# Layer 0's first expert block moved into the plan of the first stage (two-layer adaLN kernel with routed experts, one core)

## The chip, the cores and the metric

The kernel runs on one core of one Trainium2 chip. The metric is the device time of one execution in microseconds; the time given for a kernel is the median of several runs.

## The reference, cut to what matters

Two layers, each with a modulated layer norm, a mixing step, a second modulated layer norm and a feed-forward step that sends each token to two of eight experts. The change concerns the feed-forward step of layer 0:

```python
h = _layernorm(x, axis=-1) * (1 + cb) + sb          # x is (4, 1024, 256)
logits = jnp.einsum('bsd,de->bse', input_emb, Wr) + br
route_w = jax.nn.softmax(logits, axis=-1)
_, topk_idx = jax.lax.top_k(route_w, TOP_K)          # TOP_K = 2 of E = 8
...
h = jax.nn.relu(jnp.einsum('bsd,edh->ebsh', input_emb, W1) + b1[:, None, None, :])
expert_out = jnp.einsum('ebsh,ehd->ebsd', h, W2) + b2[:, None, None, :]
return jnp.einsum('bse,ebsd->bsd', routed, expert_out)
```

All is float32; D is 256, the hidden width H is 1024.

## The kernel before, in words

**First stage.** Tokens lie in tiles of 128 rows. For four batches the kernel does layer 0's norms and mixing and the routing; normed rows are stored to a table in device memory, `h_rows`, with two more columns for where a row's result goes (`store` and `mark` in `second_half`, plan pieces of SyncE, L1310 and L1323, with planned costs of 4.0 and 1.0).

**Sorting the pairs.** A token and one of its experts is a pair. Pairs of an expert fill blocks of 128 rows; there are at most 71 blocks. At the end of the first stage `total_staged` (L558) sums pairs by expert on TensorE; `close_staged` (L585) turns these totals on VectorE into numbers of blocks and the expert of each block; `across` (L685) spreads them over partitions with one product on TensorE; `limits` (L690) and `list_weights` (L716) make from that the bounds of every block and the list of weight rows. Which 128 rows are a block's is found by `reach` (L746, VectorE), `look` (L761, TensorE) and `find` (L774, VectorE); `fetch` (L791) then gathers those rows from `h_rows` with an indirect DMA that GpSimd issues. Block 0 needs no closing: `begin` (L577) gives its bound from the bases alone. Its expert is always the last one, whose weights lie in the buffers from early on.

**A block** is: gather the rows, two transposes on TensorE (`turn_rows`, L1675), a copy of the result from PSUM (`rows_turned`, L1681, VectorE), eight tiles of 128 hidden features in two groups of four (`hidden`, L1692, TensorE), each group followed by four relu with bias on ScalarE (`rectified`, L1707), eight products that sum into one PSUM tile (`values`, L1717), the bias (`biased`, L1730, VectorE) and a scatter of the rows (`kept`). Weights come in by indirect gathers (`weights_in`, `weights_out`), two buffers each, one block ahead; they are skipped when the buffer has the expert already.

**What sets the order.** Each engine runs its instructions in the order in which the program gives them. In the first stage that order is a planner's (class `Plan`, L41): each piece has an engine, a planned cost in microseconds, pieces that it comes after, slots that it holds (PSUM and SBUF buffers) and a rank. The planner steps through planned time and gives each free engine the ready piece of lowest rank; a piece from another engine counts 0.12 later; `lag` is added to a piece's end for those that wait on it. It may hold a piece back for one of a much lower rank that is ready soon. Pieces are then emitted in the order of their planned starts. `kept_busy` (L919) adds filler products on TensorE whose result nobody reads, of the highest ranks: three after look(0), five after across, three after look(1).

**The loop.** After the plan, blocks run in a loop written out by hand (L1781): in pass j the weights of block j+1, the scatter of block j-2, the gather of block j+2, `reach` for j+3, `hidden` and `rectified` for block j, transposes and copy for block j+1, `look` and `find` for j+3, then `values` and `biased` of block j-1. Ahead of it stand the gathers of blocks 0 and 1 and the transposes and copy of block 0.

In the first stage's tail the pieces are, in the code's order (L1398 to L1437):

```python
d = plan(DVE, 3.9, lambda: g0.close_staged(pa), after=[m], holds=[ps], rank=-1.0)
...
begun = plan(DVE, 0.3, g0.begin, after=[bs], rank=-1.6)
...
r = plan(DVE, 0.5, reach, after=[d] if j else [begun], rank=first)
m = plan(PE, 0.25, look, after=[r], holds=[ps], rank=first)
plan(DVE, 0.6, find, after=[m], holds=[ps], rank=first if j else -0.95)
```

Of the kernel before, what the change touches and what calls it, by code (L numbers as in the profile page):

```python
# [8 lines left out]
F32 = mybir.dt.float32  # L9
F16 = mybir.dt.float16  # L10
I32 = mybir.dt.int32
AF = mybir.ActivationFunctionType
ALU = mybir.AluOpType
# [6 lines left out]
P = 128  # L20
B, S, D = 4, 1024, 256
NC = S // P
KD = D // P
E = 8
# [115 lines left out]
def adaln_d2_kernel(  # L140
# [218 lines left out]
    class Pairs:  # L359
# [222 lines left out]
            )  # L582
            nc.vector.tensor_copy(self.nth[:, 0:1], lane)

        def close_staged(self, scratch):  # L585


            J, blocks, runs, origin, up1 = self.J, self.blocks, self.runs, self.origin, self.up1
            begin2 = float(J - LATE)

            def t(shape, what, dt=F32):
                return scratch.tile(shape, dt, tag=f"g_{what}", name=f"g_{what}", bufs=1)

# [4 lines left out]
            )  # L598
            blocks_i = t([P, 2, E], "blocks_i", I32)
            nc.vector.tensor_scalar(blocks_i, whole, 7, None, ALU.logical_shift_right)  # L600
            nc.vector.tensor_copy(blocks[:, :, 1:], blocks_i)

            up = t([P, 2, E + 1], "up")
            nc.vector.tensor_tensor_scan(
# [299 lines left out]
    sT1 = silu_of(1, c1)  # L904
    gate_rows = pa.tile([B, 2, D], F32, name="gate_rows", bufs=1)

    plan = Plan(p1=3, p2=2, pm=3, xn1=5, h1T=2, xn2=6, h2T=2, t1=1, le=2)
    PE, ACT, DVE, POOL = "PE", "ACT", "DVE", "POOL"
    tiles = {}
# [299 lines left out]
    def second_half(b):  # L1209
# [73 lines left out]
        for gs in routed:  # L1283
            k, at = 4 * len(gs), 4 * gs[0] * B + b
            tag = (b, gs[0])

            def route(k=k, at=at, tag=tag):
                g0.route(pa, tiles["pl", tag[0], tag[1]][:, :, :E], br_sb, at, k, B)

            d = plan(  # L1290
                DVE,
                0.24 * 14 + 0.16 * 4 if k == NC else 0.22 * 14,
                route,
                after=[ready[g][0] for g in gs],
                holds=[ready[gs[-1]][1]],
                rank=rank - 0.2,
            )
            for g in gs:
                of_batch["route", b, g] = d

            def mark(k=k, at=at):
                first = at - at % B
                nc.sync.dma_start(
                    h_rows[first * P : (first + k * B) * P, D:].rearrange(
                        "(c b p) d -> b p c d", b=B, p=P
                    )[at % B],
                    g0.meta[:, at : at + (k - 1) * B + 1 : B, :],
                )

            plan("SP", 1.0, mark, after=[d], rank=rank)  # L1310
            for g in gs:
                back, slot, key = backs[g]

                def store(g=g, key=key):
                    at = 4 * g * B * P
                    nc.sync.dma_start(
                        h_rows[at : at + 4 * B * P, :D].rearrange(
                            "(c b p) d -> b p c d", b=B, p=P
                        )[b],
                        tiles["xn", key],  # L1320
                    )

                plan("SP", 4.0, store, after=back, holds=[slot], rank=rank)  # L1323


    ps = plan.slot("p1")
# [75 lines left out]
        tiles["bases"] = g0.bases(ps_1)  # L1402

    m2 = plan(PE, 0.2, bases, after=[d], holds=[ps2], rank=-1.6)
    d = plan(DVE, 3.9, lambda: g0.close_staged(pa), after=[m], holds=[ps], rank=-1.0)
    bs = plan(
        ACT,
        0.25,
# [3 lines left out]
        rank=-1.6,  # L1412
    )
    begun = plan(DVE, 0.3, g0.begin, after=[bs], rank=-1.6)
    ps = plan.slot("p1")
    m = plan(PE, 0.4, lambda: g0.across(ps_1), after=[d], holds=[ps], rank=-1.0)
    kept_busy(1.1, [m], 30.0)
    d = plan(DVE, 1.4, lambda: g0.limits(pa), after=[m, bs], holds=[ps], rank=-1.0)
    plan(DVE, 1.2, lambda: g0.list_weights(pa), after=[d], holds=[ps], rank=-0.75)
    for j in range(AHEAD):  # L1420
        ps = plan.slot("p1")

        def reach(j=j):
# [8 lines left out]
        first = -1.0 + 0.1 * j if j else -1.6  # L1432
        r = plan(DVE, 0.5, reach, after=[d] if j else [begun], rank=first)
        m = plan(PE, 0.25, look, after=[r], holds=[ps], rank=first)
        plan(DVE, 0.6, find, after=[m], holds=[ps], rank=first if j else -0.95)
        if j < AHEAD - 1:
            kept_busy(0.7, [m], 30.0 + j)  # L1437
    with tc.manual_schedule(engines=ORDERED):
# [233 lines left out]
            ts.append(plan(ACT, 0.67, out_, after=[m], holds=[ps, slotT], rank=rank - 0.03))  # L1672
        return slot, slotT, hs, ts

    def turn_rows(j):  # L1675
        pt = psum(ps_m, [P, KD, P], "pm_x")
        for k in range(KD):
            nc.tensor.transpose(pt[:, k, :], xgbuf[j % 4][:, k * P : (k + 1) * P], ident)  # L1678
        return pt

    def rows_turned(pt):  # L1681
        xT = work.tile([P, KD, P], F32, tag="xT", name="xT", bufs=3)
        nc.vector.tensor_copy(xT, pt)  # L1683
        return xT

    def weights_in(j):
        gather(w1buf[j % 2], W1, g0.wrow[:, j : j + 1], E * P - 1)

    def weights_out(j):
        gather(w2buf[j % 2], W2, g0.wrow[:, j : j + 1], E * P - 1)  # L1690

    def hidden(j, xT, m4):  # L1692
        w1 = w1buf[j % 2]
        p1 = psum(ps_1, [P, 4, P], "p1_h")
        for i in range(4):
            m = 4 * m4 + i
            for k in range(KD):
                nc.tensor.matmul(  # L1698
                    p1[:, i, :],
                    lhsT=w1[:, k * H + m * P : k * H + (m + 1) * P],  # L1700
                    rhs=xT[:, k, :],
                    start=(k == 0),
                    stop=(k == KD - 1),
                )
        return p1

    def rectified(j, hid, p1, m4):  # L1707
        for i in range(4):
            m = 4 * m4 + i
            nc.scalar.activation(  # L1710
                hid[:, m, :],
                p1[:, i, :],
                AF.Relu,
                bias=w1buf[j % 2][:, KD * H + m : KD * H + m + 1],
            )

    def values(j, hid):  # L1717
        w2 = w2buf[j % 2]
        p2 = psum(ps_2, [P, D], "p2_y")
        for m in range(KH):  # L1720
            nc.tensor.matmul(  # L1721
                p2,
                lhsT=hid[:, m, :],
                rhs=w2[:, m * D : (m + 1) * D],
                start=(m == 0),
                stop=(m == KH - 1),
            )
        return p2

    def biased(j, p2):  # L1730
        y = work.tile([P, D], F32, tag="y", name="y", bufs=3)
        nc.vector.tensor_tensor(y, p2, w2buf[j % 2][:, KH * D :], ALU.add)  # L1732
        return y

    dests, ys0 = {}, {}

    def aimed(j):
        dests[j] = g0.aim(work, xgbuf[j % 4], j)

    def kept(j):  # L1740
        put("g0", dests[j], ys0[j])

    def new_hidden():
        return work.tile([P, KH, P], F32, tag="hid", name="hid")


    loads = []
    for k in range(KD):
        loads += [(a[:, k, :], w[k * P : (k + 1) * P, :]) for a, w in ((a0, fw0), (a2, fw2))]
# [24 lines left out]
            nc.sync.dma_start(*loads[j - 8])  # L1774

    with tc.manual_schedule(engines=ORDERED | {EngineType.SP}):
        for j in range(2):
            g0.fetch(xgbuf[j], h_rows, j)
        xT, hid = rows_turned(turn_rows(0)), None
        aimed(0)  # L1780
        for j in range(turning):  # L1781

# [4 lines left out]
                weights_out(j)  # L1787
            g0.fetch(xgbuf[(j + 2) % 4], h_rows, j + 2)
            reached = g0.reach(work, j + AHEAD)
            new = new_hidden()  # L1790
            for m4 in range(2):
                rectified(j, new, hidden(j, xT, m4), m4)

            xT = rows_turned(turn_rows(j + 1))
            aimed(j + 1)
            g0.find(work, g0.look(ps_m, reached), j + AHEAD)
            if j:
                ys0[j - 1] = biased(j - 1, values(j - 1, hid))
            hid = new
            once(j)  # L1800
# [767 lines left out]
```

## Time and profile before

| what | value |
|---|---|
| median of 3 runs | 1121.61 us (1121.43 to 1122.06) |
| the profiled execution: its time | 1141.97 us |
| the profiled execution: its span, first to last instruction | 1140.2 us |
| mean granted TensorE clock | 0.986 |
| TensorE busy | 1086.3 us, 95% of the span |
| VectorE, ScalarE, GpSimd busy | 592.0, 428.6, 422.5 us |
| first stage ends, the loop begins | about 115 us |

All times below are from the profiled execution and count from the start of its span. In the profile PE is TensorE, PEld its weight loads, DVE VectorE, ACT ScalarE, POOL GpSimd, SP SyncE; L12 is line 12 of the kernel. A row of the timeline has start, length, engine, line, operation, what it writes and reads, and in brackets how long the engine had been idle and what ended that. A row of stretches has from and to, its length, then for each engine the busy time and the number of instructions, then the granted clock, the DMA engines' mean busy share and GB/s.

### The profile page before, as it was taken

The numbers are of one execution on the slowest core, as the hardware profiler recorded it, in microseconds if no ns is written. First come the engines' busy times: TensorE is split into PE (matmuls) and PEld (weight loads), VectorE is DVE, ScalarE is ACT, GpSimd is POOL, SyncE is SP. The second block draws the span as 40 slices with busy tenths as digits, with TensorE's granted clock in tenths as the row PEclk, the third lists the DMA queues.
The fourth block names the chain that finished last, engine by engine and source line by source line (L and its number), as shares of the span: only waits on it lengthen the run. The fifth ranks groups of instructions, "written<-read, shape, count | busy, mean of one in ns | idle before, by whom it ended". The sixth has DMA issues, their size and how long they took to land. (4 is left out here: it accounts for less than half of the span.)

```text
span 1140.2 us, 18501 instructions
## 1 busy us (share of the span) xinstructions
PE 1086.3 (95%) x6238; PEld 847.0 (74%) x6238; DVE 592.0 (52%) x2308; ACT 428.6 (38%) x1164; POOL 422.5 (37%) x483
## 2 busy tenths in 40 slices
PE   8998999999999999999999999999999999899883
PEld 5894999999999999999988466566576575547641
DVE  7787232222222222222274788975776445888456
ACT  5976333322333323233343343432434235333421
POOL 1000455555555555555543011010044233616452
PEclk8999999999999999999999999999999999999996
DMA  9414549242422415151260312100024223323532
GB/s 321 174 31 103 191 156 302 100 153 75 154 78 75 150 39 192 33 193 40 70 223 27 96 34 83 39 10 19 19 62 129 75 82 103 102 88 107 155 118 93
DMA packets 77693, 122.38 MB, mean 107 GB/s; under 512 B 27340, under 2 KB 57301, under 8 KB 72990
## 3 DMA queue, kind: packets, MB, share of 16 engines
q0 software_dynamic: 31872, 69.68, 19.5%
q1 hardware_dynamic: 44622, 49.92, 13.3%
q10 hardware_dynamic: 1104, 1.58, 0.4%
q8 instruction: 52, 0.85, 0.3%
q14 instruction: 43, 0.35, 0.1%
HBM read 205.25 MB, written 30.22 MB: 207 GB/s over the span
## 5 line engine op out<-in xcount | busy, mean ns | idle before, releaser
L1710 ACT ACTIVATE hid<-p_h,w 128x128 f32<-128x128 f32 x544 | 154.8, 368 | 323.5 <-issue 251.9
L1698 PEld LDWEIGHTS p_h<-xT,w 128*128 128x128 f32 x2176 | 253.2, 192 | 7.2 <-DVE xT L1683 1.9
L1698 PE MATMUL p_h<-xT,w 128*128 128x128 f32 x2176 | 254.7, 275 | 3.1 <-DVE xT L1683 2.7
L1721 PE MATMUL p_y<-w,hid 128*128 128x256 f32 x1088 | 249.0, 382 | 0.2 <-issue 0.2
L2007 PE MATMUL p_u<-hT,a 128*128 128x512 f32 x512 | 232.0, 596 | 2.9 <-ACT hf L2019 1.4
L1721 PEld LDWEIGHTS p_y<-w,hid 128*128 128x128 f32 x1088 | 201.6, 190 | 25.1 <-DMA w<-in_W,g_wrow 0.4
L2007 PEld LDWEIGHTS p_u<-hT,a 128*128 128x128 f32 x512 | 93.5, 190 | 100.5 <-issue 89.7
L347 POOL DMA_INDIRECT w<-in_W,g_wrow x134 | 135.1, 1008 | 77.4 <-ACT hid L1710 46.7
L1683 DVE COPY xT<-pm_x 128x256 f32<-128x256 f32 x68 | 28.8, 424 | 187.0 <-PE pm_x L1678 134.4
L812 POOL DMA_INDIRECT y<-y,g_dest x68 | 69.5, 1022 | 143.5 <-DVE g_reached L752 108.4
L2055 PE MATMUL p_f<-a,hf 128*128 128x256 f32 x512 | 116.7, 380 | 2.0 <-DVE step L2096 1.0
L1732 DVE TENSOR_TENSOR y<-p_y,w 128x256 f32<-128x256 f32 x68 | 28.9, 425 | 166.9 <-PE p_y L1721 160.7
L2055 PEld LDWEIGHTS p_f<-a,hf 128*128 128x128 f32 x512 | 95.9, 190 | 20.8 <-issue 5.9
L347 POOL DMA_INDIRECT xg<-h_rows,g_row x68 | 66.7, 980 | 120.4 <-DVE g_row L787 98.9
L2103 POOL TENSOR_TENSOR x_sb<-x_sb,step 128x256 f32<-128x256 f32 x32 | 24.9, 778 | 205.8 <-DVE step L2096 153.6
L2315 PE MATMUL p_e<-ew,xT 128*128 x280 | 71.5, 386 | 0.8 <-ACT y L2325 0.8
L2019 ACT ACTIVATE hf<-p_u,decay 128x512 f32<-128x512 f32 x56 | 38.2, 685 | 74.9 <-PE p_u L2007 63.5
L347 POOL DMA_INDIRECT xg<-ga_rows,ga_row x39 | 37.3, 956 | 54.1 <-DVE g_hits L778 19.3
L2315 PEld LDWEIGHTS p_e<-ew,xT 128*128 128x128 f32 x280 | 49.0, 190 | 11.0 <-issue 3.8
L2023 DVE SCALAR_TENSOR_TENSOR hf<-p_u,decay,hf 128x512 f32<-128x512 f32 x56 | 41.9, 748 | 25.7 <-PE p_u L2007 14.3
L1618 DVE TENSOR_TENSOR h<-h,mod 128x256 f32<-128x256 f32 x128 | 51.6, 425 | 6.8 <-ACT h L1608 4.1
L2325 ACT COPY y<-p_e 128x256 f32<-128x256 f32 x70 | 26.1, 373 | 51.4 <-PE p_e L2315 19.2
(371 smaller groups left out, 1259.1 us busy)
## 6 DMA issues: line engine op xcount, KB each, us to landing
yg<-y SPq DMA_DIRECT2D x32, 256.0 KB
ga_y<-y SPq DMA_DIRECT2D x39, 128.0 KB
x_sb<-in_x SPq DMA_DIRECT2D x8, 512.0 KB
h_rows<-xn SPq DMA_DIRECT2D x8, 512.0 KB
gb_y<-y SPq DMA_DIRECT2D x31, 128.0 KB
out_x<-x_sb SPq DMA_DIRECT2D x7, 512.0 KB
a<-in_fw SPq DMA_DIRECT2D x6, 512.0 KB
mod<-mod_rows SPq DMA_DIRECT2D x6, 512.0 KB
```

The source lines that it names most:

```text
L347: return nc.gpsimd.indirect_dma_start(out=dst, out_offset=None, in_=table, in_offset=bass.IndirectOffsetOnAxis(ap=index, axis=0), bounds_c ...
L812: nc.gpsimd.indirect_dma_start(out=table, out_offset=bass.IndirectOffsetOnAxis(ap=dest, axis=0), in_=y, in_offset=None, bounds_check=2 * s ...
L1618: nc.vector.tensor_tensor(h, h, mods1[(sc, sh)[i]][:, b, :], (ALU.mult, ALU.add)[i])
L1698: nc.tensor.matmul(p1[:, i, :], lhsT=w1[:, k * H + m * P : k * H + (m + 1) * P], rhs=xT[:, k, :], start=(k == 0), stop=(k == KD - 1),)
L1710: nc.scalar.activation(hid[:, m, :], p1[:, i, :], AF.Relu, bias=w1buf[j % 2][:, KD * H + m : KD * H + m + 1],)
L1721: nc.tensor.matmul(p2, lhsT=hid[:, m, :], rhs=w2[:, m * D : (m + 1) * D], start=(m == 0), stop=(m == KH - 1),)
L1732: nc.vector.tensor_tensor(y, p2, w2buf[j % 2][:, KH * D :], ALU.add)
L2007: nc.tensor.matmul(pu, lhsT=a[:, k, m * P : (m + 1) * P], rhs=made["n1", c, "hT"][:, k, :, :], start=(k == 0), stop=(k == KD - 1),)
L2019: nc.scalar.activation(made[key, m], made[key, m, 0], AF.Silu, scale=decays[c])
L2023: nc.vector.scalar_tensor_tensor(h, made[key, m, 1], decays[c], h, ALU.mult, ALU.mult)
L2055: nc.tensor.matmul(made[key, "p2", b], lhsT=made[key, m][:, b * P : (b + 1) * P], rhs=a1[:, m, :], start=(m == 0), stop=(m == KH - 1),)
L2315: nc.tensor.matmul(made[key, "p2"], lhsT=made[key, "xT"][:, k, :], rhs=ew_flat[:, bass.ds(made[key, "at"] + k * D, D)], start=(k == 0), st ...
```

## The change

`close_staged` is cut in two: its first three instructions become `whole_blocks`, a piece of its own. `find(0)` gets rank -1.6, and the rest of the closing waits for both. Block 0's gather, transposes, copy (now on ScalarE), hidden products in four pieces, relu in two and values in two become pieces of the first stage's plan (`first_block`); so does block 1's gather. Block 0's gather waits for all stores to `h_rows`. Its hidden tile and transposed rows lie in two buffers of the first stage. The helpers `turn_rows` to `new_hidden` move up in the file; `hidden` and `values` can be given a part. The loop loses what is done already: the two gathers, block 0's transposes, hidden, rectified and values; `biased(0)` stays in pass 1.

```diff
-        def close_staged(self, scratch):
...
+        def whole_blocks(self, scratch):
...
-            nc.vector.tensor_copy(blocks[:, :, 1:], blocks_i)
+            nc.vector.tensor_copy(self.blocks[:, :, 1:], blocks_i)
+
+        def close_staged(self, scratch):
...
-    d = plan(DVE, 3.9, lambda: g0.close_staged(pa), after=[m], holds=[ps], rank=-1.0)
+    whole = plan(DVE, 0.45, lambda: g0.whole_blocks(pa), after=[m], holds=[ps], rank=-1.0)
...
+    def first_block(found):
+
+        slots = [plan.slot("xn1") for _ in range(2)]
+        kept0 = tiles["first"] = {}
+        rows = plan(
+            POOL, 1.0, lambda: g0.fetch(xgbuf[0], h_rows, 0), after=[found, *stores], rank=-1.6, lag=1.9
+        )
+        ps = plan.slot("pm")
+
+        def turn():
+            kept0["pt"] = turn_rows(0)
...
+        m = plan(PE, 0.35, turn, after=[rows], holds=[ps, *slots], rank=-1.5)
+        h = plan(ACT, 0.45, lambda: nc.scalar.copy(kept0["xT"], kept0["pt"]), after=[m], holds=[ps, *slots], rank=-1.5)
+        done = []
+        for m4 in range(2):
+            ps = plan.slot("p1")
+            for part in range(2):
...
+                h = plan(PE, 0.9, mm, after=[h], holds=[ps, *slots], rank=-0.6)
+            done.append(
+                plan(
+                    ACT,
+                    1.1,
+                    lambda m4=m4: rectified(0, kept0["hid"], kept0[m4], m4),
...
+        for part in range(2):
...
+            m = plan(PE, 1.75, mm, after=[m, done[part]], holds=[ps, *slots], rank=-0.5)
+
     for j in range(AHEAD):
+        if j == 1:
+            closed = plan(
+                DVE, 3.5, lambda: g0.close_staged(pa), after=[whole, found], rank=-1.0
+            )
+            ps = plan.slot("p1")
+            m = plan(PE, 0.4, lambda: g0.across(ps_1), after=[closed], holds=[ps], rank=-1.0)
+            kept_busy(1.1, [m], 30.0)
+            d = plan(DVE, 1.4, lambda: g0.limits(pa), after=[m, bs], holds=[ps], rank=-1.0)
+            plan(DVE, 1.2, lambda: g0.list_weights(pa), after=[d], holds=[ps], rank=-0.75)
         ps = plan.slot("p1")
...
-        plan(DVE, 0.6, find, after=[m], holds=[ps], rank=first if j else -0.95)
+        found = plan(DVE, 0.6, find, after=[m], holds=[ps], rank=first)
+        if j == 0:
+            first_block(found)
+        elif j == 1:
+            plan(
+                POOL,
+                1.0,
+                lambda: g0.fetch(xgbuf[1], h_rows, 1),
+                after=[found],
+                rank=-1.5,
+                lag=1.9,
+            )
...
-        for j in range(2):
-            g0.fetch(xgbuf[j], h_rows, j)
-        xT, hid = rows_turned(turn_rows(0)), None
+        xT, hid = None, None
...
-            new = new_hidden()
-            for m4 in range(2):
+            new = new_hidden() if j else None
+            for m4 in range(2 if j else 0):
                 rectified(j, new, hidden(j, xT, m4), m4)
...
-            if j:
+            if j == 1:
+                ys0[0] = biased(0, tiles["first"]["p2"])
+            elif j:
                 ys0[j - 1] = biased(j - 1, values(j - 1, hid))
```

## The prediction, before the changed kernel was run

> **What bounds the kernel now.** I read the page first (engines, then the clock row), then TensorE's waits inside the block loop, then the timeline around the hand-over from the first stage to the loop, then busy time in stretches cut where the clock changes. The page:
>
> ```profile
> PE 1086.3 (95%) x6238; PEld 847.0 (74%) x6238; DVE 592.0 (52%) x2308; ACT 428.6 (38%) x1164; POOL 422.5 (37%) x483
> PEclk8999999999999999999999999999999999999996
> ```
>
> TensorE (PE) is busy 95% of the span; its clock is full but for the first slice and the end. TensorE's waits from 128 to 600 us, the block loop:
>
> ```profile
> PE p_h L1698 <- DVE xT L1683: 1.2, 1, 1.2
> PE p_h L1698 <- ACT hid L1710: 0.2, 1, 0.2
> ```
>
> Those are the two longest: 472 us with under 2 us of waiting. So the loop is TensorE from end to end, and what the hand-over gains or loses, measured where block 2 starts, is carried on whole. The hand-over (start us, us, engine, line):
>
> ```profile
> 105.33 0.23 DVE L580 TENSOR_SCALAR g_limit<-g_base,g_others 128x2 f32<-128x2 f32 x1 [1.99 <-ACT g_base L481]
> ...
> 105.92 0.17 DVE L596 TENSOR_SCALAR g_whole<-pm_total 128x16 int32<-128x16 f32 x1
> ...
> 106.22 0.29 PE L765 MATMUL pm_counts<-g_more,g_reached 128*128 128x129 f16 x2
> ...
> 106.44 1.02 PE L1382 MATMUL pm_mod<-wmod,sT 128*4 128x512 f32 x2
> 106.68 0.20 DVE L604 TENSOR_TENSOR_SCAN g_up<-g_again,g_blocks 128x18 f32<-128x18 f32 x1
> ...
> 109.82 0.48 PE L688 MATMUL pm_blocks<-g_diagonal,ones 128*128 128x142 f32 x2 [1.61 <-DVE g_filled L649]
> ...
> 110.48 1.12 POOL L347 DMA_INDIRECT xg<-h_rows,g_row  x1 [98.86 <-DVE g_row L787]
> ...
> 112.81 0.82 PE L915 MATMUL pm_busy<-busy 128*128 128x512 f16 x3 [0.32 <-DVE g_row L787]
> ...
> 113.47 0.43 PE L1678 MATMUL pm_x<-ident,xg 128*128 128x128 f32 x2
> ...
> 114.48 0.42 DVE L1683 COPY xT<-pm_x 128x256 f32<-128x256 f32 x1
> ```
>
> To see: the closing runs on VectorE (DVE) from 106.68 to 109.68, the sum across follows at 109.82, row 0 is only then found and gathered (110.48), the transposes come at 113.47 behind three filler products (L915), and block 0's products start at 115.01. Idle TensorE time lies between. Stretches cut at the clock's own changes (us, then PE busy, PEld busy, ..., granted clock third from the end):
>
> ```profile
> 17.14:20.55 3.41, 1.64 (x11) 1.24 (x11) 3.19 (x12) 3.41 (x7) 0.00 (x0) 1.00 1.12 360
> 20.55:23.96 3.41, 2.76 (x11) 2.08 (x12) 3.00 (x17) 2.43 (x6) 0.00 (x0) 0.50 0.89 352
> 23.96:27.37 3.41, 3.41 (x18) 3.41 (x17) 3.17 (x14) 3.11 (x7) 0.00 (x0) 0.50 0.89 328
> ...
> 1071.91:1075.32 3.41, 1.96 (x23) 1.15 (x22) 0.00 (x0) 0.65 (x2) 1.89 (x2) 1.00 0.45 136
> ```
> ```profile
> 109.31:112.72 3.41, 2.28 (x11) 1.10 (x11) 3.09 (x19) 0.00 (x0) 1.12 (x1) 1.00 0.12 34
> ```
>
> A stretch with 1.64 of 3.41 busy (48%) was followed by half clock for two stretches; one with 81% busy did not end it, a full one did. One with 57% kept the clock. The hand-over's stretches (2.32, 2.28 and 2.21 busy, 65 to 68%) keep it too, thanks to eleven filler products.
>
> **What the Trainium skill says.** "TensorE: Matmul & The Clock Gate", Part 1: The HAM clock gate, What's actually happening: activity in free-running windows of 3413 ns decides between half and full clock. The trace agrees: the drop lasts 6.83 us, two windows. How much work makes a window idle it doesn't say; here it lies between 48% and 57%. Same page, Architectural detail: the array is 16× 32×32: TensorE runs products in program order, only weight loads are pulled ahead, and VectorE is a strict queue. The filler ahead of the transposes shows it. "DMA: Bandwidth & Descriptors", Anatomy of one DMA: about 2.0 us plus bytes over 436 GB/s, so 2.3 us for a row gather of 132 KB; the trace has 2.98 from issue to transposes (110.48 to 113.46), and I use that.
>
> **Where the planner puts the new pieces.** The order on each engine is the planner's. On its own clock (costs written in the code, no measured times) the totals' product ends at 108.49. From there: whole blocks 0.45, begin 0.3, reach 0.5, look(0) (after the last piece of the layer 1 modulation, which now starts first), find(0) ends at 111.20, the closing (3.5) at 114.70, across at 115.22, limits at 116.74, look(1) and look(2) at 118.11, the last filler at 119.16. The gather waits for *all* stores, each 4.0 on the planner's clock: SyncE's (SP) tail from 102.75 is 4+1+1+4+4, ending at 116.75. So the gather is placed at 116.87 and the transposes, 1.0+1.9 later, at 119.89: **behind across, both looks and all fillers in TensorE's queue**, though the rows will be there early.
>
> **The change part by part.**
> 1. *Whole blocks ahead of begin.* The three instructions take 0.66 (105.92 to 106.58), so reach(0) ends at 106.65, not 106.01. look(0) now stands behind the modulation's last piece: 105.26 plus four passes of 0.43 gives 106.98; with its 0.29, 107.27.
> 2. *find(0) ahead of the closing.* It takes 0.54 (109.66 to 110.20) and ends at 107.85. It used to lie under the sum across, at no cost. The gather is issued at about 108.1, 2.4 us earlier. The stores have landed (DMA share falls to 0.02 at 107), so that wait costs nothing; nothing is queued behind it on POOL, where gather 1 follows only after find(1). Rows arrive at 111.1.
> 3. *The closing* starts at 107.85 instead of 106.68: **+1.17** for it, across, limits, look(1), find(1) and the filler that needs find(1)'s buffer.
> 4. *Transposes* behind that filler: 113.47 + 1.17 = 114.64, ended 115.05. *The copy* goes to ScalarE (ACT), idle here: 0.37 (the 128x256 copy of L2325) plus 0.05 and 0.06 of hand-over; it no longer stands behind find(2) and the weight list on VectorE. Products start at 115.53 against 115.01: **+0.52**.
> 5. *values(0)* moves from behind the transposes of block 2 to directly behind hidden(0), 3.5 us either way; its ScalarE step is done in time (products' start +3.3 and +5.0). But it covered the copy of block 2's xT: transposes to next products take 0.90 when nothing lies between (118.65 to 119.55) and 0.33 when values do (123.23 to 123.56): **+0.57**.
> 6. *biased(0)*, the early gather 1 and the fetches: at nothing, under TensorE. Weight gathers: block 2's waits for block 0's relu, issued at 120.8 (was 120.26), landed 5.5 later by the transfer seen after 120.26; needed at 128.1. Block 3's moves most: relu(1) ends near 128.7 instead of 124.57, landing at 134.5 against 135.5. Cover of 1.0; if gone, each us is paid.
>
> Sum without a clock change: +0.52 + 0.57 = **+1.1 us** (0.6 to 1.8, by how soon look(0) runs).
>
> 7. *The clock.* TensorE's fillers still end at 108.2, but across now starts at 110.99, not 109.82: the idle gap grows from 1.6 to 2.8 us. The stretch 109.31 to 112.72 holds 110.99 to 112.55, 1.56 busy: **46%**, under the 48% that lost the clock. For window edges between 110.0 and 113.1 (3.1 us of the 3.41 there are) it is 50% or less. Half clock from 112.72: looks, three fillers and transposes cost about 0.9 more; products from 116.45 to 119.55 run at half rate, 1.55 lost; **+2.4**, or +4.1 if the window that starts with a short gap doesn't count as busy, as at 20.55. Other edges give 3.2 to 3.8. Lower bound: zero, if no drop. I take **+3.3**.
>
> Sum: 1.1 + 3.3 = +4.4 us on the profiled execution's 1141.97 (span 1140.2); the median of the runs is 1121.61, 0.982 of it, so +4.3: **1125.9 us** (1125.0 to 1126.7).
>
> **Rivals.**
> *No clock drop*, only the reordering: 1121.61 + 1.1 = 1122.7 (1122.2 to 1123.4). For it: one drop near the threshold is thin evidence, and the edges are free-running. Against: no stretch at or under 49% kept a full clock in this trace.
> *Transposes early* (faster): if they stand ahead of across in TensorE's queue, they run at 111.1, hidden(0) at 112.0, values end at 119.5, block 2 starts at 125.0 instead of 127.07: -2.1, 1119.5, and no drop. It decides if the planner has the gather before about 111.7, that is, if its stores end there and not at 116.75.
> *Worse still*: memory of the first stage, now read until values(0) ends near 122, is reused by tiles that VectorE clears on entering the loop (114.2 to 115.4); parked there, VectorE delays the next copy by 0.9; or block 3's weights are late by over 1.0. With the drop: 1127 to 1128.
>
> **Chances.** Clock drop 0.57, no drop 0.27, early transposes 0.09, worse 0.07. About 0.2% (2.24 us) is what a measurement of this kernel can tell from no change: faster 0.09, same 0.27, slower 0.64. The range reaches from the no-drop case to just over the drop's upper bound: 1122.2 to 1127.2; the drop alone has 1125.0 to 1126.7.
>
> **What would show it.** Right: row 0's gather at about 108, transposes after the third group of fillers near 114.6, across near 111.0, a granted clock of 0.5 for two or three windows from about 110 to 113 on, block 2's products 4 us later. Wrong: transposes before across; a clock that stays at 1.0 (then block 2 starts near 128.2); or idle time at block 3's products for weights.

## The result, and the profile after

The changed kernel took 1122.32 us (median of 22 runs, 1119.79 to 1125.31) against 1120.67 us of the kernel before beside it (22 runs, 1117.94 to 1122.83). The ratio is 1.0015, 95% interval 1.0008 to 1.0022: 1.7 us slower (0.9 to 2.5), inside the 0.2% that the text before set as the mark of "same". Forecast were 1125.9 us, 4.3 slower; the measured time lies at the lower edge of the forecast's overall range (1122.2 to 1127.2).

Two things are needed to read what follows. First, chips differ: the kernel before took 1143.53, 1142.56 and 1141.29 us in the three timed batches of experiments below, each on another chip. So only runs of one batch are compared, by their ratio. The profile of before (span 1140.2) belongs to that slower kind and the one of after (1120.7) to the faster. The 20 us between them are not spread over the run. Started from the span's beginning, after is 1.47 us later than before through the whole block loop, 1.32 at 840 us, 0.3 at 962, then 5.8 earlier at 1025 and 19.6 earlier at 1119. A scale of 0.982 on the loop was the wrong picture, though it moved the forecast by only 0.1.

Second, moments of the hand-over are counted here from the start of the totals' product (`pm_total`, 105.02 us into the span before, 104.88 after), so that profiles of different chips can be laid over each other.

The page of the changed kernel, engines and clock:

```profile
PE 1078.1 (96%) x6238; PEld 846.5 (76%) x6238; DVE 588.5 (53%) x2307; ACT 430.2 (38%) x1165; POOL 423.9 (38%) x483
PEclk8999999999999999999999999999999999999997
```

TensorE is still what the span consists of. Forty slices are too coarse for a drop of a few microseconds; the timeline of the hand-over, of the changed kernel, is where to look:

```profile
105.23 0.17 DVE L591 TENSOR_SCALAR g_whole<-pm_total 128x16 int32<-128x16 f32 x1 [2.03 <-PE pm_total L569]
106.93 0.29 PE L770 MATMUL pm_counts<-g_more,g_reached 128*128 128x129 f16 x2
107.73 0.18 DVE L609 TENSOR_TENSOR_SCAN g_up<-g_again,g_blocks 128x18 f32<-128x18 f32 x1
109.14 1.12 POOL L347 DMA_INDIRECT xg<-h_rows,g_row  x1 [98.19 <-DVE g_runs L630]
110.85 0.48 PE L693 MATMUL pm_blocks<-g_diagonal,ones 128*128 128x142 f32 x2 [2.98 <-DVE g_filled L654]
113.83 0.82 PE L921 MATMUL pm_busy<-busy 128*128 128x512 f16 x3 [0.32 <-DVE g_row L792]
114.49 0.38 PE L1425 MATMUL pm_x<-ident,xg 128*128 128x128 f32 x2
114.91 0.37 ACT L1514 COPY xn<-pm_x 128x256 f32<-128x256 f32 x1 [7.15 <-PE pm_x L1425]
115.33 3.84 PE L1446 MATMUL p_h<-xn,w 128*128 128x128 f32 x32 [0.46 <-ACT xn L1514]
119.01 3.62 PE L1470 MATMUL p_y<-w,xn 128*128 128x256 f32 x16
122.66 0.24 DVE L380 COPY ga_meta<-twice 128x16 f32<-128x16 f32 x1 [7.44 <-PE p_y L1470]
123.38 0.42 DVE L1430 COPY xT<-pm_x 128x256 f32<-128x256 f32 x1
123.85 3.84 PE L1446 MATMUL p_h<-xT,w 128*128 128x128 f32 x32
128.43 3.84 PE L1446 MATMUL p_h<-xT,w 128*128 128x128 f32 x32 [0.40 <-DVE xT L1430]
```

The order is the one forecast: transposes (L1425) behind the sum across, the looks and the last fillers (L921). The row at 122.66 is outside the forecast's sum; only its rival "worse still" had it. VectorE stood for 7.44 us until the last product of block 0's values was done, and the copy of block 1's rows (123.38) came behind it. Busy time in stretches cut at the clock's own windows, same kernel (columns as before: PE first, granted clock third from the end):

```profile
105.78:109.19 3.41, 2.09 (x8) 0.41 (x6) 2.41 (x16) 0.72 (x2) 0.05 (x1) 1.00 0.17 39
109.19:112.61 3.42, 1.56 (x7) 0.72 (x7) 2.58 (x16) 0.00 (x0) 1.07 (x1) 1.00 0.15 41
112.61:116.02 3.41, 2.45 (x15) 1.56 (x16) 2.48 (x16) 0.37 (x1) 1.61 (x2) 1.00 0.09 18
```

The middle stretch has 1.56 of 3.42 us busy, 46%, the very figure that the forecast held too little. The clock stayed at 1.00.

The profiles over each other, in us since the totals' product began. "Products of block 2" is where the loop takes over. Most later differences stay; the last column shows where they did not, since block 4's rows came late in some executions.

| kernel | row 0's gather | across | transposes of block 0 | its products | products of block 2 | products of block 4 |
|---|---|---|---|---|---|---|
| before | 5.46 | 4.80 | 8.45 | 9.99 | 22.05 | 36.88 |
| before, again (e9) | 5.47 | 4.80 | 8.45 | 9.99 | 22.05 | 36.88 |
| after | 4.26 | 5.97 | 9.61 | 10.46 | 23.55 | 38.48 |
| after, again (e11) | 4.56 | 6.02 | 9.66 | 10.51 | 23.60 | 38.72 |
| after, again (e6) | 5.34 | 5.99 | 10.24 | 11.09 | 24.19 | 39.12 |
| after, again (e10) | 5.55 | 6.03 | 10.44 | 11.28 | 24.39 | 39.32 |
| e1, no fillers in the gaps | 5.22 | 5.99 | 8.50 | 9.59 | 24.71 | 39.77 |
| e2, the gap filled | 3.74 | 5.98 | 9.62 | 10.47 | 23.57 | 39.12 |
| e3, memory of its own | 5.27 | 5.98 | 9.63 | 10.47 | 23.08 | 38.52 |
| e4, find(0) behind the closing | 5.30 | 4.64 | 8.31 | 9.21 | 22.31 | 37.50 |
| e5, thin fillers | 5.65 | 5.98 | 9.38 | 10.51 | 25.02 | 40.84 |
| e7, rows used early | 4.93 | 5.98 | 7.91 | 8.81 | 21.69 | 36.62 |
| e7 once more (e12) | 4.35 | 5.98 | 7.34 | 8.23 | 21.52 | 36.44 |
| e8, and block 1's transposes early | 5.27 | 5.99 | 8.24 | 9.14 | 21.41 | 37.06 |

After is 1.50 behind at block 2, and 1.61 from block 3 on. That is nearly all of the 1.7 measured (0.9 to 2.5).

### The profile page after: what moved, and what is told of

It reads as the page before. It is cut to its first block, busy times and chain, and to the rows that moved or that the text cites. A ratio compares the mean times of both kernels' runs of the same rounds, so it can differ in the third digit from the quotient of the medians.

```text
span 1120.7 us, 18499 instructions
## 1 busy us (share of the span) xinstructions
PE 1078.1 (96%) x6238; PEld 846.5 (76%) x6238; DVE 588.5 (53%) x2307; ACT 430.2 (38%) x1165; POOL 423.9 (38%) x483
## 5 line engine op out<-in xcount | busy, mean ns | idle before, releaser
L1446 PEld LDWEIGHTS p_h<-xT,w 128*128 128x128 f32 x2144 | 249.4, 192 | 6.6 <-DVE xT L1430 3.5
L1446 PE MATMUL p_h<-xT,w 128*128 128x128 f32 x2144 | 250.7, 275 | 2.8 <-DVE xT L1430 2.7
L1470 PE MATMUL p_y<-w,hid 128*128 128x256 f32 x1072 | 245.3, 382 | 0.0
L1470 PEld LDWEIGHTS p_y<-w,hid 128*128 128x128 f32 x1072 | 198.7, 190 | 24.3
L347 POOL DMA_INDIRECT xg<-ga_rows,ga_row x39 | 37.5, 962 | 52.9 <-DVE g_hits L783 19.6
```

Of the source, the lines that this page charges most:

```text
L347: return nc.gpsimd.indirect_dma_start(out=dst, out_offset=None, in_=table, in_offset=bass.IndirectOffsetOnAxis(ap=index, axis=0), bounds_c ...
L1446: nc.tensor.matmul(p1[:, i, :], lhsT=w1[:, k * H + m * P : k * H + (m + 1) * P], rhs=xT[:, k, :], start=(k == 0), stop=(k == KD - 1),)
L1470: nc.tensor.matmul(p2, lhsT=hid[:, m, :], rhs=w2[:, m * D : (m + 1) * D], start=(m == 0), stop=(m == KH - 1),)
```

## The experiments

The theory on trial was the forecast's own: a window of TensorE that is at most about 48% busy loses the clock, and that costs 2.4 to 4.1 us. The first rival: the clock mostly holds, and what is lost is order and waiting, among it VectorE parked on reused memory. A second rival, formed on the first profile: the clock looks not at the profile's busy time but at how long TensorE really streams columns. Busy time counts the tail of a lone product too: look(0), two products of 129 columns, is busy for 0.29 us in after, of which by the reckoning below it streams 0.11. I take the streamed time from the traces: sixteen products of 256 float32 columns start 3.46 us before what follows them (119.01 to 122.46, rounded), 0.84 ns per column; a filler of 512 half-precision columns takes 0.216 (14 of them 3.18, five 1.24), half of that per column. Summed over a window and divided by 3.41 us this is called its **streamed share** below.

**e1, no fillers in the gaps.** All eleven filler products of the changed kernel's tail go: those after look(0), after across and after look(1).

```diff
-            kept_busy(1.1, [m], 30.0)
...
-        if j < AHEAD - 1:
-            kept_busy(0.7, [m], 30.0 + j)
```

> The changed kernel without the eleven filler products of the hand-over (3 after look(0), 5 after across, 3 after look(1)); what is computed stays. My prediction's theory (a window under about half busy loses the clock): from the end of look(0) near 107.1 to block 0's products TensorE has only the sum across, four looks and two transposes, about 1.6 us of work in 8 us, so the trace shows a granted clock of 0.5 for two or three windows in the hand-over, and the kernel is 2 to 4 us slower than the changed kernel, 1.0035 to 1.005 of before. Rival (the clock holds here, the fillers only cost their place in the queue): clock 1.0 throughout, transposes about 0.65 us earlier since they no longer stand behind three fillers that wait for find(1)'s buffer, block 2's products near 127.8 instead of 128.43, 1.0009 of before.

Measured: 1.0014 of before (1.0004 to 1.0023), less than the 1.0035 to 1.005 expected. The clock dropped. Stretches of e1:

```profile
108.03:111.44 3.41, 0.48 (x2) 0.30 (x2) 2.53 (x16) 0.00 (x0) 1.12 (x1) 1.00 0.01 2
111.44:114.86 3.42, 2.06 (x10) 1.49 (x11) 3.16 (x19) 0.37 (x1) 0.95 (x1) 0.50 0.14 39
114.86:118.27 3.41, 3.41 (x18) 3.41 (x18) 0.00 (x0) 0.45 (x2) 1.98 (x2) 0.50 0.25 58
118.27:121.68 3.41, 3.41 (x24) 3.18 (x24) 0.00 (x0) 1.84 (x7) 0.37 (x1) 1.00 0.07 24
```

A window with 14% busy is followed by two at 0.50; the first of them, 60% busy, did not bring the clock back, the second, full, did. Block 0's 32 products then took 5.86 us. The timeline of e1:

```profile
114.00 5.86 PE L1446 MATMUL p_h<-xn,w 128*128 128x128 f32 x32 [0.46 <-DVE g_expert L731]
```

Without fillers they began 0.87 earlier than in after (9.59 against 10.46) and block 2's began 1.16 later: a price of 2.03 for the drop, which is 5.86 less 3.84. So what the forecast described exists and costs 2 us when two windows are lost. The question is how often the changed kernel meets it.

**e2, the gap filled.** Fourteen filler products after look(0) where there were three, so that the gap ahead of across is covered.

```diff
-            kept_busy(0.7, [m], 30.0 + j)
+            kept_busy(0.7 if j else 3.2, [m], 30.0 + j)
```

> The changed kernel with 14 filler products instead of 3 after look(0), which reach over the idle stretch from 107.9 to 110.1 and end ahead of the sum across (110.85); nothing else moves. If some executions of the changed kernel lose the clock in that gap (their spread is 1119.8 to 1125.3, with mean clocks of 0.987 to 0.993), these become rarer: the median falls by about 0.7 us and no execution stands 2.5 us over the others. Rival (the gap is harmless): the same as the changed kernel, 1.0015 of before, with as wide a spread. The trace's place of block 2's products should be 128.4 in both.

Measured: 1.0002 (0.9991 to 1.0012). The hand-over kept the clock and reached block 2 at 23.57, as after did without fillers there. Taking every risk of a drop away gains nothing over an execution of after that had none. The expected narrowing did not come: 13 executions spread from 1141.4 to 1146.4. One drop was there all the same, earlier in the plan (stretches of e2):

```profile
94.53:97.94 3.41, 1.91 (x14) 1.18 (x12) 2.93 (x16) 3.15 (x8) 0.00 (x0) 1.00 0.17 11
97.94:101.36 3.42, 3.42 (x27) 2.68 (x28) 0.81 (x6) 2.11 (x5) 0.00 (x0) 0.50 0.30 80
```

The first row is 56% busy and lost the clock; after's 46% had kept it. So the profile's busy share does not decide. The streamed share puts them in the right order: 0.36 here, 0.38 there. The drop does not belong to e2's fillers: e9, the kernel before, lost the clock at the same place (56% busy, half clock from 98.04 us), and its totals' product began at 106.06 us instead of 105.02. A drop there is outside the table, which counts from that product.

**e5, thin fillers.** The same filler lists with 64 columns in place of 512 and more products, meant to keep TensorE busy in the profile while it streams little.

```diff
+    def thin(us):
...
+        for _ in range(int(us / 0.095)):
+            nc.tensor.matmul(
+                pb[:, :64], lhsT=busy16[:, :P], rhs=busy16[:, :64], start=True, stop=True
+            )
```

> The changed kernel with the hand-over's fillers made of products of 64 columns instead of 512 (7, 11 and 7 of them, in the same places), so that TensorE shows about as much busy time but streams far fewer columns. Reading after the first traces: the clock follows columns streamed through the array (dropped at 36% of a 3.41 us window and less, kept at 37% and more), not the busy share of the profile. Then this kernel loses the clock in the hand-over at any position of the window (streamed share under 25%), block 0's products stretch from 3.7 to over 5 us, and it is 1 to 2 us slower than the changed kernel. Rival (busy share decides, and 46% is enough): clock 1.0 in the hand-over as in the changed kernel, same time.

Measured: 1.0023 (1.0007 to 1.0039), the clock at 0.50 for two windows from 110.94, block 0's products 5.25 long, block 2 at 25.02. But the run does not separate the two measures. Thin products follow each other so fast that the lists took 0.36 to 0.55 us, and the window ahead of the drop was 20% busy and 16% streamed: poor by either. It confirms e1, no more.

**e6, e9, e10, e11: both kernels again.** The changed kernel three times more (e6 timed) and the kernel before once more, with nothing edited, since whether a free-running window falls badly is a matter of each execution.

> The changed kernel once more, beside the others on this chip and at another position of the free-running window. If the streamed share decides, about 7 positions in 10 hold a window at 36% or less (reckoned by sliding the window over the changed kernel's trace; for the kernel before it is 1 in 4), so a drop to 0.5 in the hand-over is likelier than not here, and the median is 1.0015 of before. If the clock always holds, the trace looks as the first one did.

> The kernel before once more, for a profile beside those of the changed kernel. The clock of the hand-over: if the share of a window in which TensorE streams columns decides (drops seen at 36% and less, kept at 37% and more), about one execution in four of this kernel has a window poor enough there, so most likely the clock stays at 1.0; if the profile's busy share decides (48% and less), it never drops here, since no position of the window has under 50% busy. The late part of layer 0, 560 to 612 us from the start: if block waits of about 1 us for a copy that stands behind VectorE's combine belong to this kernel, they are here again; if they belonged to one execution, TensorE waits for nothing there.

> The changed kernel once more, the same on every engine. Streamed share: about two executions in three drop the clock in the hand-over. If dropped for one window, block 2's products start 0.6 to 0.7 us later after the totals' product than the 23.55 us of the first profile without a drop; if for two windows, about 2. Busy share, as forecast: a drop in nearly all executions, for two windows, with 2.4 to 4.1 us.

> The same once more. Each theory expects what it expects of the run before; a drop in neither, or in both, would still fit a share of two in three, and a count of all profiles of this kernel is what is wanted: with 0.6 to 2 us lost in the executions that drop and nothing in the others.

Measured: e6 1.0005 of before (0.9989 to 1.0021), so this batch does not show the slowdown by itself. e6 and e10 dropped the clock in the hand-over; e11 did not, nor did e9. Stretches of e10:

```profile
106.50:109.92 3.42, 0.89 (x6) 0.27 (x5) 2.77 (x18) 0.72 (x2) 0.00 (x0) 1.00 0.09 12
109.92:113.33 3.41, 2.91 (x9) 1.48 (x10) 2.20 (x11) 0.00 (x0) 1.12 (x1) 0.50 0.14 41
113.33:116.74 3.41, 2.47 (x19) 1.73 (x17) 1.87 (x12) 0.37 (x1) 1.97 (x2) 1.00 0.14 39
```

A poor window (26% busy), one window at 0.50, and full clock again at 113.33, before block 0's products begin. In e10's timeline they have their usual length:

```profile
110.42 0.81 PE L693 MATMUL pm_blocks<-g_diagonal,ones 128*128 128x142 f32 x2 [3.04 <-DVE g_filled L654]
111.03 2.34 PE L921 MATMUL pm_busy<-busy 128*128 128x512 f16 x5
115.68 3.84 PE L1446 MATMUL p_h<-xn,w 128*128 128x128 f32 x32 [0.46 <-ACT xn L1514]
```

Only across (0.81 long against 0.48), five fillers (2.34 against 1.24) and the first of the looks ran slow. Block 2 came at 24.39, 0.84 behind after; in e6 at 24.19, 0.64 behind. Two of four executions of the changed kernel thus dropped, at 0.74 on the mean. e9's loop wait is taken up under e7.

Over all fourteen traces (before, after and the twelve experiments), in layer 0 and where the clock was full, every window with a streamed share up to 0.36 was followed by half clock (18 of 18, busy shares from 0.14 to 0.56). Of those from 0.37 to 0.39, seven kept the clock and one (e11, at 17.74 us, 54% busy) lost it; from 0.41 up none lost it. Sliding a window over the traces, a streamed share of at most 0.36 is met in the hand-over in 25% of the positions in before, 70% in after, all in e1 and e5, none in e2. The share was worked out after the fact from these very traces, and some matmul records can be missing, so 0.36 is a reading, not a law. What is shown is that 46% busy kept and 56% busy lost the clock.

**e3, memory of its own.** Block 0's hidden tile and transposed rows in the loop's pool instead of the first stage's buffers.

```diff
-            hid, both = [
-                pa.tile([P, 4, D], F32, tag="xn1", name="xn1", bufs=plan.room["xn1"])
-                for _ in range(2)
-            ]
+            hid = pw.tile([P, 4, D], F32, name="hid0")
+            both = pw.tile([P, 1, D], F32, name="xT0")
```

> The changed kernel with block 0's hidden tile and transposed rows in memory of their own, not in first-stage buffers that the next stage's tiles take over. Theory: VectorE is then no longer held from 115.2 to 122.6 by values(0); the copy of block 1's rows follows its transposes at once, and block 1's and block 2's products start 0.5 us earlier (block 2 at 127.9 instead of 128.4); 1.001 of before. Rival (VectorE's wait was for TensorE's transposes anyway): block 2 stays at 128.4.

Measured: 1.0008 (0.9994 to 1.0021), the clock kept. The timeline of e3:

```profile
122.78 0.38 PE L1425 MATMUL pm_x<-ident,xg 128*128 128x128 f32 x2
123.20 0.42 DVE L1430 COPY xT<-pm_x 128x256 f32<-128x256 f32 x1 [6.50 <-PE pm_x L1425]
139.82 0.41 PE L1425 MATMUL pm_x<-ident,xg 128*128 128x128 f32 x2 [0.32 <-issue]
```

VectorE now waits for the transposes themselves and copies 0.42 after they start; in after it was 0.92 (122.46 to 123.38). Products of block 1 start 0.89 after the transposes (123.67), not 1.39, and block 2 comes at 23.08, 0.47 sooner. The parking is real and costs 0.5 at block 2. In this execution the gain did not last: TensorE stood idle ahead of block 4's transposes (last row), and block 4's products came at 38.52, where after has 38.48. The same gap is in e2, e4, e5 and e8, which lost 0.26 to 0.89 from block 3 to block 4, and in e11 with 0.19; in e5 and e8 the trace names the gather of the rows as its end. The gather is issued 6.4 us ahead of where after needs the rows (28.23 to 34.64), and in e5 and e8 its rows were used only 7.3 and 7.1 us after the issue. So what removing the parking is worth in the end depends on that gather. The time's interval is too wide to show it.

**e4, find(0) behind the closing.** The rest of the change stays, but the closing no longer waits for the first search, and find(0) has its old rank.

```diff
-                DVE, 3.5, lambda: g0.close_staged(pa), after=[whole, found], rank=-1.0
+                DVE, 3.5, lambda: g0.close_staged(pa), after=[whole], rank=-1.0
...
-        found = plan(DVE, 0.6, find, after=[m], holds=[ps], rank=first)
+        found = plan(DVE, 0.6, find, after=[m], holds=[ps], rank=first if j else -0.95)
```

> The changed kernel with find(0) put back behind the closing (rank -0.95, the closing waits for the whole blocks alone); block 0 stays in the plan. Theory (row 0's early search only delays the chain, as the transposes stand behind looks and fillers): across 1.1 us earlier (near 109.75), transposes near 113.4, block 0's products near 114.3, block 2 near 127.4, within 0.05% of before. Rival (block 0's rows set the start): row 0's gather goes from 109.1 to about 110.5, transposes stay at 113.5 or later behind it, and block 2 gains less than 0.5 us.

Measured: 0.9991 (0.9979 to 1.0002). The timeline of e4:

```profile
108.67 0.48 PE L693 MATMUL pm_blocks<-g_diagonal,ones 128*128 128x142 f32 x2 [1.65 <-DVE g_filled L654]
112.34 0.44 PE L1425 MATMUL pm_x<-ident,xg 128*128 128x128 f32 x2
113.24 3.84 PE L1446 MATMUL p_h<-xn,w 128*128 128x128 f32 x32 [0.46 <-ACT xn L1514]
```

Across is 1.33 earlier than in after and everything behind it as well: transposes 1.30, block 2 1.24. Block 0's gather, issued at 5.30 here and at 4.26 in after, makes no difference. Seeking row 0's rows ahead of the closing is therefore 1.24 of the 1.50 lost: the gather bought early is not used early, and the closing pays for it. With the order put back the rest nearly balances. Products 0.78 sooner than before by the ScalarE copy, 0.57 lost on the uncovered copy, 0.49 on the parking: +0.28, and 22.31 less 22.05 is 0.26 (0.62 at block 4, behind its late rows).

**e7, rows used early.** So: keep find(0) early, and let the planner believe the rows early as well. The last stores are planned at 1.2 instead of 4.0 and the gather's lag at 3.6, so that the transposes are ordered ahead of the later looks; looks 1 and 2 write the other PSUM slot so that nothing blocks them; e2's fillers and e3's memory come with it. The computation is whole.

```diff
-                stores.append(plan("SP", 4.0, store, after=back, holds=[slot], rank=rank))
+                stores.append(plan("SP", 1.2 if (b, g) in ((3, 0), (3, 1), (1, 1)) else 4.0, store, after=back, holds=[slot], rank=rank))
...
-            POOL, 1.0, lambda: g0.fetch(xgbuf[0], h_rows, 0), after=[found, *stores], rank=-1.6, lag=1.9
+            POOL, 1.0, lambda: g0.fetch(xgbuf[0], h_rows, 0), after=[found, *stores], rank=-1.6, lag=3.6
...
-            kept_busy(1.1, [m], 30.0)
+            kept_busy(0.7, [m], 30.0)
-        ps = plan.slot("p1")
+        ps = plan.slot("pm" if j else "p1")
...
-        if j < AHEAD - 1:
-            kept_busy(0.7, [m], 30.0 + j)
+        if j == 0:
+            kept_busy(3.2, [m], 30.0)
```

> The changed kernel with block 0's rows used as soon as they come: the planner is told 1.2 instead of 4.0 for the last three stores, so it places the transposes behind across but ahead of both looks; a filler of 14 ahead of across, one of 3 between across and the transposes, none later; looks 1 and 2 use another PSUM pool; block 0's tiles have memory of their own. Theory (the place of the transposes in TensorE's queue is what the change lacks): gather at 108 to 109, transposes at 111.5 to 112.2, block 0's products near 113.0, block 2's near 125.9 against 128.4 in the changed kernel and 127.1 before: 0.9985 of before. Rival (the chain through row 1 or the weights of block 2 takes over): block 2 at 127 or later, and no gain over before.

> The version with its rows used early once more (leaves nothing out of the computation), for the part of its gain that did not come from the hand-over. There it led the kernel before by 0.36 us where block 2 starts, yet it was 2.4 us faster in time; TensorE's wait of 1.0 to 1.6 us for the copy behind VectorE's combine at 560 to 612 us, there in all profiles of before and of after, was absent. If that belongs to this version: no such wait in this profile either, and a time 0.998 of before's. If it belonged to that one execution: a wait of about 1 us is here, and the profile's lead over before falls to under 1 us after 612 us; the ratio may then be nearer to 0.9997, which 0.36 us alone would give.

Measured: 0.9983 of before (0.9969 to 0.9996); once more, in e12, 0.9976 (0.9967 to 0.9985), 1138.70 against 1141.29 us. Both are faster than before, which after never was. The timeline of e7:

```profile
110.48 0.48 PE L693 MATMUL pm_blocks<-g_diagonal,ones 128*128 128x142 f32 x2 [0.61 <-DVE g_filled L654]
110.80 0.81 PE L921 MATMUL pm_busy<-busy 128*128 128x512 f16 x3
112.41 0.44 PE L1425 MATMUL pm_x<-ident,xg 128*128 128x128 f32 x2 [0.80 <-DMA xg<-h_rows,g_row]
113.31 1.16 PE L1446 MATMUL p_h<-xT,w 128*128 128x128 f32 x8 [0.46 <-ACT xT L1512]
114.31 0.40 PE L770 MATMUL pm_counts<-g_more,g_reached 128*128 128x129 f16 x4
```

The transposes wait for nothing but the rows, and the looks run between block 0's products instead of ahead of them. That is the forecast's rival of early transposes, with one difference: they stand behind across, not ahead. Block 2 comes 0.36 sooner than before, in e12 0.53; some 1.2 us had been expected.

This is not the 2 to 2.7 us of the timing. It does not even last: behind gaps of 0.2 and 0.3 us ahead of block 55's transposes the lead is down to 0.03 and 0.12. In the profiles a new lead arises after that, at the end of the loop. TensorE's waits from 560 to 612 us in e9 (before), and below that in e7:

```profile
PE p_h L1698 <- DVE xT L1683: 1.6, 2, 1.0
PE pm_x L1678 <- issue: 0.3, 1, 0.3
```

```profile
PE pm_x L1425 <- issue: 0.2, 1, 0.2
```

There a copy of rows stands behind VectorE's combining of layer 0's results (`yg`), which waits for its loads. The wait is in all six traces of before and after and in e1, e3, e4, e5, 0.7 to 1.6 at its longest, and in none of e2, e7, e8, e12. In e12 TensorE has 1.0 of another kind there ("issue"). Across this stretch e7 gains 2.8 us on the first profile of before and e12 1.5; but e9, before again, gains 0.8 on it too, and e4, which has the wait, 1.8. The loads wait for scatters: in before, after, e1, e3 and e4 they are issued 12.9 to 13.3 us after the scatter at about 558, in e2, e7, e8 and e12 11.2 to 11.5, but in e5, which has the wait, 11.1 as well. So earlier loads alone do not remove it, and why e7 and e12 are faster in time is open. What e2, e7, e8 and e12 have in common is the fourteen fillers 450 us earlier, and I know of nothing that would carry from there; no run took it apart.

**e8, and block 1's transposes early.** e7, with block 1's transposes and copy in the plan, between the two halves of values(0), to cover that copy again.

```diff
+            m1 = plan(PE, 0.35, turn1, after=[rows], holds=[ps], rank=-0.55)
+            plan(ACT, 0.45, copy1, after=[m1], holds=[ps], rank=-0.7)
...
-            xT = rows_turned(turn_rows(j + 1))
+            xT = rows_turned(turn_rows(j + 1)) if j else tiles["xT1"]
```

> As the run before, and block 1's transposes and copy (on ScalarE) stand in the plan too, between the two halves of values(0), so that their latency is covered. Theory: it takes off the idle time ahead of block 1's products, 0.6 us: block 2's products near 125.3; 0.998 of before. Rival: row 1's gather isn't landed in the middle of values(0), TensorE waits there, and block 2's place is that of the run before or later.

Measured: 0.9981 (0.9971 to 0.9991), no better than e7. It leads e7 by 0.28 at block 2 and has lost that and more two blocks on, where block 4's rows come late. The timeline of e8:

```profile
134.12 3.73 PE L1446 MATMUL p_h<-xT,w 128*128 128x128 f32 x32
138.38 0.41 PE L1425 MATMUL pm_x<-ident,xg 128*128 128x128 f32 x2 [0.53 <-DMA xg<-h_rows,g_row]
```

Against before it is 0.53 ahead at block 3 and 0.19 behind at block 4, 0.72 given back. It is the wait for block 4's rows, at the place where TensorE stood idle in e2 to e5 too.

## Why the prediction was wrong, step by step

**Step 7, the clock, is the step that failed.** It took +3.3 us, from the rule that at most 48% of busy time in a window loses the clock, for a window of 46% and for nearly all positions of it. Measured: 46% kept the clock in after, 46% in e3 and e4, 47% in e11. The drop came in two of four executions, through other window positions, with 16 and 26% busy. Its price was 0.64 and 0.84, where 2.4 to 4.1 stood: the window at half clock ended before block 0's products, so that of the forecast's two parts only the "about 0.9" for looks, fillers and transposes was paid, and not the 1.55 on the products nor the 1.7 for a second window. Mean over executions: half of 0.74, about 0.4. A higher price exists (2.0 in e1; in e5 block 0's products alone took 1.4 more), but only after a window that is nearly empty and a next one that is poor as well. The flaw is that one drop at 48% was taken for a threshold of busy time and weighed at 0.57. That window streamed for only 0.35 of its length; after's, with 46% busy, streamed for 0.38.

**The sum without the clock, +1.1 (0.6 to 1.8): right in mechanism, 0.4 short.** Measured +1.50 at block 2 in after and 1.55 in e11.

- *1, whole blocks first:* right. look(0) was forecast to start at 106.98 and started at 106.93.
- *2, find(0) early:* the rows were asked for at 109.14, not at 108.1. That stores' wait was put down at nothing because the DMA share had fallen by 107; the profile after has 128 GB/s up to 107 and none from 107 to 109, and the gather was still held until 109.14. That the stores held it is inferred: the piece comes after find(0), whose index was ready at 107.81, and after the stores. The Trainium skill describes such a wait for GpSimd's transfers: "DMA: Bandwidth & Descriptors", Anatomy of one DMA, SWDGE (gpsimd) path, puts most of the fixed 2 us down to the wait for the receipt of the write, heaviest into device memory. About 2 us lie between the last bytes (107.0) and the release here too, but the stores come from SyncE's queue, which that section is not about, and no run isolated it. Without consequence in after, where the transposes stood behind other work.
- *3, the closing +1.17:* right. Across moved from 4.80 to 5.97; e4 undoes it with 1.33.
- *4, transposes and copy, +0.52:* right, 0.47. Forecast were transposes at 114.64 and products at 115.53; they came at 114.49 and 115.33.
- *5, the uncovered copy, +0.57:* right. In e3, with the parking gone, block 2 is 23.08 less 22.05, 1.03 behind, of which 0.48 had been there at the products: 0.55.
- *6, gathers at nothing:* right in after, e6 and e10, where the loop keeps its distance from 134 us on, but with luck. The weights never made TensorE wait there; the rows of block 4, whose cover the forecast did not reckon, have 6.41 us from issue to use (6.89 in before), and e11 waited 0.19 for them.
- *The parking of VectorE* was named in the rival "worse still", at 0.9 and, with late weights, a chance of 0.07. It happened, for 0.49 (e3). It belonged in the sum, and it is the 0.4 that the sum is short: that a tile's memory is used until 122 and written on entering the loop can be read off the code.

**The rivals.** "No clock drop", 1122.7 us (1122.2 to 1123.4) with a chance of 0.27, is what came, in time (1122.32) and mostly in cause: 0.47 + 0.57 + 0.49 is 1.5, some 0.4 more from drops in some executions make 1.9, and 1.7 (0.9 to 2.5) was measured. Before has such drops too, by the sliding window in a quarter of the positions; what they cost there no run shows, and it would bring the 1.9 down. "Transposes early" was dismissed on the right ground, the planner's 4.0 for stores, and e7 shows that the hand-over gains as soon as that ground is taken away, though 0.4 to 0.5 at block 2 and not 2.1, and little of it lasts.

## What to carry to other kernels

A transfer that is started earlier is worth nothing until its first reader also moves; look at what is queued ahead of that reader on its own engine before giving up anything (here 1.2 us of VectorE) for the earlier start. A gain at the front is kept only if the next transfers have cover to spare; follow it some blocks on. Do not take the busy share of a window as the clock's measure when the window holds lone products: price a possible drop by how many executions meet it and by which instructions lie in the slow window, with the profile repeated. When work is moved across the border of two stages, ask which memory it holds and who writes that next.

## What the runs showed of the hardware

- Half clock lasted one window (3.41 us) or two (6.83). The busy share of the first of them does not say which: 83% ended it after one in e4 and e12, 84% in after (20.44 to 23.86) and 89% in e11 (21.15 to 24.56) did not. Streamed share, reckoned afterwards with each column taking twice as long, sorts the cases in layer 0: 0.74 and more ended it after one window, 0.72 and less did not. "TensorE: Matmul & The Clock Gate", Part 1: The HAM clock gate, of the Trainium skill, gives the window of 3413 ns and half clock after an idle one; the lengths agree, but the windows that lost the clock here were not idle: up to 56% busy and 39% streamed.
- The same program took 1138.11 (a single run), 1141.29, 1142.56 and 1143.53 us on four chips, and 1120.67 us in the first batch, whose chip is not on record. In the profiles compared the difference lay after about 960 us, not in the block loop.
